# A two-layer graph network on one core: seams rearranged, the first linear layer one product later, adjacency transposes spread out

## The chip, the core and the metric

The kernel runs on one core of a Trainium2 chip. The core has five engines that run at the same time, each with its own queue: TensorE (PE) for matrix products, VectorE (DVE), ScalarE (ACT) and GpSimd (POOL) for elementwise work, SyncE (SP), which here only issues DMAs. They meet at semaphores. PE writes into PSUM, eight banks of 128 partitions x 512 fp32 numbers; everything else lies in SBUF or in device memory. The metric is the time of one launch in microseconds (us); lower is better.

## What is computed

Sixteen batches b of x (1024 nodes x 256 features), one adjacency matrix (1024 x 1024), all fp32, two layers. Cut from the reference:

```python
# layer 0
fea = transpose(x); c = mean(x, axis=features); diff = c[None, :] - c[:, None]
A = abs(abs(sigmoid(diff) - 0.5) - 0.5) * 2.0        # 1024 x 1024 per batch
g = relu((fea @ (adj * A_s)) * para)                  # A_s: A made symmetric
q = transpose(g); k, v = split(x @ kv_w)              # 4 heads of 64
x = layernorm(x + softmax(q @ k.T * scale) @ v)
# layer 1
A_hat = D^-1/2 (adj + I) D^-1/2
agg = A_hat-weighted sum of x over the nodes
h = relu(batchnorm(agg @ W1.T + b1))                  # 256 -> 512
o = batchnorm(h @ W2.T + b2)                          # 512 -> 256
x = layernorm(x + o)
```

The batch norms of layer 1 take their statistics over all batches and nodes. So the first linear layer must be done for all sixteen batches before the second starts, and the second for all before the final layernorm.

## The kernel before

`fast_path` does all the work, in stages that follow each other on PE:

- **Prologue.** Batch 0 is transposed, and keys, values and the row of node means are formed. `prologue(b)` returns three lists of closures (`first`, `steps`, `side`): `first` begins with `begin` (on DVE `csum`, `ccol`, `ncol`; two DMAs on SP that bring the means back as a row `crow`) and goes on with four transposes of x (`transpose_x`); `steps` holds the key and value products (L864, L877), and `side` the graph weights (L808, L813, L817).
- **Attention.** Sixteen batches of sixteen *bursts* (u = 0 to 15, about 3.4 us of PE each). A burst is two units of scores (`ps`, L924), exponentials on ACT (L929), and the outputs (`po`, L945) of the burst before. Between the bursts, lists called `sums` (`normalise`), `full` (`residual`), and `late` (`statistics_x1`, `finish_x1`: the layernorm) are drained at fixed values of u, and so is the next batch's prologue. In the last batch there is no next prologue; the dictionary `last` puts the preparation of layer 1 in its place: `transpose_adjacency(m, h)` (four transposes into a PSUM tile `pah`, copied by ACT into `ahT`, L1071 and L1074), `degrees`, `transpose_weights` (`pw`), `add_identity`, `scale_adjacency` (DVE, L1096).
- **`aggregate_first`** (L1123) aggregates batch 0 right after, into two PSUM tiles `pagg`. PSUM in this stage has tiles of three kinds, `tile_s` (two banks), `tile_t` and `tile_o` (one bank each).
- **Layer 1 loop**, b = 1 to 15: `aggregate(b)` and `linear1(b-1)` are interleaved on PE. Both go by a scheme of Strassen and Winograd with seven products instead of eight. `products` writes them as p1, p6, p2, p7, p5, p4, p3 on three PSUM banks a, b and c: p1 and p2 share bank a, p6, p7 and p4 share b, p5 and p3 share c. A later product accumulates onto what lies in its bank, after ACT or DVE has read the former value out. Aggregation has one such group of seven products per batch (3.43 us of PE each), linear has two (0.86 us a product) and statistics (L1382) after each group. The scheme needs sums of its operands beforehand: `x1_sums` makes `x1S` on POOL (L684 to L687) for the aggregation of two batches on, and `linear1(b)` first of all makes `tT` on DVE (`right_sums`, L691 to L694) from the finished `agg`.
- **Last linear**, `ph` (L1452), then the coefficients of the first batch norm, and `scale_shift1` (ACT, L1442), which applies it in place to `h`.
- **Second linear**, `po` (L1512): h is read back from device memory by `load_h` (L1497), two buffers `hl`. Evacuated by DVE (L1523), with statistics (L1527); the last tile by ACT (L1518).
- **Final stage**: `scale_shift` (ACT, L1554), the residual added on PE and DVE (L1563, L1577, L1592), statistics on DVE, the layernorm's coefficients on POOL (L1613), and `finish` (ACT, L1625, and DVE), then the output DMA (L1629).

The order on PE, ACT and DVE is written out by hand (`manual_schedule`): instructions stand in each engine's queue in the order in which Python emits them. POOL's and SP's are placed by the framework's scheduler. The loop that sets the order of layer 1:

```python
steps = aggregate(b)
for i, step in enumerate(steps):
    step()
    if i == len(steps) - 1 and b < B - 1:
        later = linear1(b)
    run_linear(lin, 2)
lin = later
```

`run_linear(lin, k)` emits the next k linear products; statistics and the store of h (POOL) come with the product that they follow. With two a step, steps 0 to 6 get p1 p6 | p2 p7 | p5 p4 | p3 p1 | p6 p2 | p7 p5 | p4 p3.

Of the kernel before, what the change touches and what calls it, by code (L numbers as in the profile page):

```python
# [18 lines left out]
P = 128  # L19
# [496 lines left out]
def fast_path(  # L516
# [208 lines left out]
    with (  # L725
# [235 lines left out]
        def normalise(b, pr):  # L961


            k = b * PAIRS + pr
            den = tile_t(f"den_{k}")
            for i in range(4):
                nc.tensor.matmul(  # L967
                    den[i * 32 : (i + 1) * 32, :], ones[:, :32],
                    G[b, pr, i // 2]["acc"][:, (i % 2) * HALF : (i % 2 + 1) * HALF],
                    start=True, stop=True,  # L970
                )
            row = rdp.tile([P, HALF], F32, tag="drow", name=f"drow_{k}")
            nc.scalar.copy(row, den)
            for i in range(4):
                nc.sync.dma_start(den_d[k][i : i + 1, :], row[i * 32 : i * 32 + 1, :])
            for qh in range(2):
                col = small.tile([P, 4, 2], F32, tag="dcol", name=f"dcol_{k}_{qh}")
                for hd in range(2):
                    i = 2 * qh + hd
                    nc.sync.dma_start(  # L980
                        col[:, :, hd], den_d[k][i : i + 1, :].rearrange("o (n p) -> p (o n)", p=P)
                    )
                G[b, pr, qh]["col"] = col

        def residual(b, pr, qh):
            g, s = G.pop((b, pr, qh)), st[b]
            k = (b * PAIRS + pr) * 2 + qh
            nc.vector.reciprocal(r_all[:, k], g["col"])
            pt = tile_t(f"poT_{k}")
            for j in range(4):  # L990
                nc.tensor.transpose(
                    pt[:, j * P : (j + 1) * P], g["oT"][:, j * P : (j + 1) * P], ident
                )
            o = rdp.tile([P, 4, 2, D], F32, tag="o", name=f"o_{k}")
            nc.vector.tensor_mul(  # L995
                o, pt.rearrange("p (n h d) -> p n h d", h=2, d=D),
                r_all[:, k].unsqueeze(3).to_broadcast([P, 4, 2, D]),
            )
            xs = s["x"][:, 4 * qh : 4 * qh + 4, pr * P : (pr + 1) * P]
            nc.gpsimd.tensor_tensor(xs, xs, o.rearrange("p n h d -> p n (h d)"), ALU.add)  # L1000
# [116 lines left out]
        def aggregate_first(m):  # L1117
            if m == 0:
                agg[0] = xTp.tile([P, CC, N], F32, tag="xT", name="agg_0")
                agg["ps"] = [tile_s(f"pagg_{c}") for c in range(CC)]  # L1120
            for c in range(CC):
                for hs in (H0, H1):
                    nc.tensor.matmul(  # L1123
                        agg["ps"][c][:, hs], x1l[0][:, m, c * P : (c + 1) * P], aht[m][:, hs],
                        start=(m == 0), stop=(m == NCH - 1),
                    )
            if m == NCH - 1:
                for c in range(CC):
                    nc.scalar.copy(agg[0][:, c, :], agg["ps"][c])
# [11 lines left out]
        with tc.manual_schedule(engines={mybir.EngineType.PE, mybir.EngineType.Activation, mybir.EngineType.DVE}):  # L1141
# [5 lines left out]
            for _ in range(8):  # L1147
                run(steps, 1)
                run(side, 2)
            run(next_first, 5)  # L1150
# [5 lines left out]
            run(next_side, 99)  # L1156
            run(next_steps, 8)
            full, sums, late = [], [], []

            def back(j):  # L1160
# [12 lines left out]
            last = {  # L1173
                0: [(transpose_adjacency, (m, h)) for m in (0, 1) for h in (0, 1)],
                4: [(transpose_adjacency, (m, h)) for m in (2, 3) for h in (0, 1)],
                6: [(transpose_adjacency, (m, h)) for m in (4, 5) for h in (0, 1)],
                8: [(transpose_adjacency, (m, h)) for m in (6, 7) for h in (0, 1)],
                5: [(load_x1l, (0,))],
                7: [(load_x1l, (1,))],
                9: [(degrees, ())],  # L1180
                10: [(transpose_weights, ())],
                12: [(add_identity, ())],
                15: [(scale_adjacency, (0,))],
            }
            before_last = {
                6: [(load_weights, ())],
# [7 lines left out]
            for j in range(len(bursts)):  # L1194
# [11 lines left out]
                if b == B - 1:  # L1206
                    if u == 0:
                        run(sums, 1)
                    elif u in (2, 4, 12):
                        run(full, 2)  # L1210
                    elif u == 5:
                        run(late, 1)
                    elif u == 7:
                        run(late, 1)
                    elif u == 8:
                        run(sums, 1)
                elif u == 0:
# [34 lines left out]
            for m in range(NCH):  # L1252
                if m + 1 < NCH:
                    scale_adjacency(m + 1)
# [5 lines left out]
            for i in range(NCH // 2):  # L1260
                adjacency_sums(i)
            run(late, 2)
# [24 lines left out]

    with (
# [5 lines left out]
        tc.manual_schedule(  # L1294
            engines={mybir.EngineType.PE, mybir.EngineType.Activation, mybir.EngineType.DVE}
        ),
# [118 lines left out]
        for b in range(1, B):  # L1415
            if b + 1 < B:
                load_x1l(b + 1)
                x1_sums(b + 1)
            else:
# [6 lines left out]
            for i, step in enumerate(steps):  # L1426
# [3 lines left out]
                run_linear(lin, 2)  # L1430
# [17 lines left out]
        for k in range(HC):  # L1448
            ps = [bank(f"ph_{k}_{half}") for half in range(2)]
            for c in range(CC):  # L1450
                for half, hs in enumerate((H0, H1)):
# [4 lines left out]
            if k == HC - 1:  # L1456
                scale_shift1(h0[0], 0)
# [6 lines left out]
        for k in range(1, HC):  # L1464
# [10 lines left out]
    with tc.tile_pool(name="o2p", bufs=1) as o2p:  # L1475
# [11 lines left out]
        with (  # L1487
            tc.tile_pool(name="hl", bufs=2) as hl,
            tc.manual_schedule(
                engines={mybir.EngineType.PE, mybir.EngineType.Activation, mybir.EngineType.DVE}  # L1490
            ),
        ):
            hs_of = {0: h0}

            def load_h(b):
                ht = hl.tile([P, HC, N], F32, tag="hl", name=f"hl_{b}")
                nc.sync.dma_start(ht, h_d[b])  # L1497
                hs_of[b] = [ht[:, k, :] for k in range(HC)]

            load_h(1)  # L1500
            for b in range(B):
                if b + 2 < B:
                    load_h(b + 2)
                if b + 1 < B:
                    for k in range(HC):
                        scale_shift1(hs_of[b + 1][k], k)
                h = hs_of.pop(b)
                for c in range(CC):
                    ps = tile_s(f"po2_{b}_{c}")
                    for k in range(HC):  # L1510
                        for hs in (H0, H1):
                            nc.tensor.matmul(  # L1512
                                ps[:, hs], w2T[:, k, c * P : (c + 1) * P], h[k][:, hs],
                                start=(k == 0), stop=(k == HC - 1),
                            )
                    if b == B - 1 and c == CC - 1:
                        for hs in (H0, H1):
                            nc.scalar.activation(  # L1518
                                o2T[b][:, c, hs], ps[:, hs], AF.Identity,
                                bias=cols["b2"][:, c : c + 1],  # L1520
                            )
                    else:
                        nc.vector.tensor_scalar(  # L1523
                            o2T[b][:, c, :], ps, cols["b2"][:, c : c + 1], None, ALU.add
                        )
                    for half, hs in enumerate((H0, H1)):
                        nc.vector.bn_stats(bn2_st[:, c, 2 * b + half, :], o2T[b][:, c, hs])  # L1527
                    if b == B - 1:
                        coefficients2(c)
                if b >= B - 3:  # L1530
                    load_x1(b - (B - 3), xp, "x")
# [7 lines left out]
        with (  # L1539
            tc.tile_pool(name="fin2", bufs=4) as fin2,  # L1540
            tc.tile_pool(name="ps_held", bufs=3, space=PSUM) as ps_held,
            tc.tile_pool(name="ps_sum", bufs=2, space=PSUM) as ps_sum,
            tc.manual_schedule(
                engines={mybir.EngineType.PE, mybir.EngineType.Activation, mybir.EngineType.DVE}
            ),
        ):
            for b in range(3, 7):
                load_x1(b, fin2, "xf")
# [20 lines left out]
            def residual2(b):  # L1569
# [27 lines left out]
                for n in range(4, NCH):  # L1597
                    nc.vector.bn_stats(st[:, n, :], held[b][:, (n - 4) * C : (n - 3) * C])

# [3 lines left out]
                pool = nc.gpsimd  # L1603
# [7 lines left out]
                pool.tensor_tensor(rstd, var, mhalf, ALU.pow)  # L1611
# [4 lines left out]
            def finish(b, rstd, nmr):  # L1616
                xt, hx = xf.pop(b), held.pop(b)
                y = o2T[b].rearrange("p c n -> p (c n)").rearrange("p (n c) -> p n c", c=C)
                for n in (0, 1):
# [4 lines left out]
                for n in (4, 5, 6, 7, 2, 3):  # L1624
# [4 lines left out]
                nc.sync.dma_start(out[b].rearrange("(n p) c -> p n c", p=P), y)  # L1629
                if b + 7 < B:  # L1630
                    load_x1(b + 7, *((fin2, "xf") if 3 <= b < 7 else (xp, "x")))
# [5 lines left out]
            for b in range(B):  # L1637
                coeffs[b] = residual2(b)
                if b + 1 < B:
                    scale_shift(b + 1)  # L1640
                if b:
                    finish(b - 1, *coeffs.pop(b - 1))
            finish(B - 1, *coeffs.pop(B - 1))


# [41 lines left out]
```

## Time and profile before

| | us |
|---|---|
| median of 3 runs (2630.56 to 2632.49) | 2630.99 |
| the profiled execution | 2630.78 |
| its span on the trace | 2628.9 |
| PE busy, of the span | 2565.4 |
| DVE busy | 1515.3 |
| ACT busy | 1202.5 |
| POOL busy | 362.0 |

The stages begin on PE at about these times of the trace: attention 78 us, its last batch 1622, `aggregate_first` 1704, layer 1 loop 1736, last linear 2286, second linear 2300, final stage 2526; the last output lands at the end of the span. One batch of the layer 1 loop lasts about 36.4 us.

The profile is read in views. The list of waits names, for each engine, what ended its idle times: the waiting group, the group that released it, the total, the number of times, the longest. A timeline gives start, duration, engine, line, operation, output and inputs by the program's names, tile shape, and in brackets how long the engine had been idle before and who ended it. Successive matmuls overlap a little in their recorded durations, so their pitch (start to start) is what they cost. A window gives the busy time of the engines in a stretch, PE, PEld (weight loads), DVE, ACT, POOL in this order, then the granted clock of PE (1.00 is full), the share of DMA time and GB/s.

### The profile page before, as it was taken

How to read it: one execution, taken by the hardware profiler on the slowest of the kernel's cores; microseconds unless marked ns; L12 is line 12 of the kernel's file. 1: busy time of each engine (PE TensorE's matmuls, PEld its weight loads, DVE VectorE, ACT ScalarE, POOL GpSimd, SP SyncE). 2: the span in 40 equal slices, each digit the busy share in tenths (PEclk: the TensorE clock that was granted, in tenths of full speed). 3: DMA queues.
4: the chain of work that ended last, by engine and by line, in shares of the span. 5: the costliest groups of instructions: out<-in, count | busy, mean ns of one | idle time of the engine just before them, and what ended most of it. 6: DMA issues, size and time to landing. Idle time of an engine off the chain costs nothing.

```text
span 2628.9 us, 32328 instructions
## 1 busy us (share of the span) xinstructions
PE 2565.4 (98%) x13158; PEld 1130.2 (43%) x13158; DVE 1515.3 (58%) x1941; ACT 1202.5 (46%) x1479; POOL 362.0 (14%) x439
## 2 busy tenths in 40 slices
PE   8999999999999999999999999999999999999986
PEld 4443443444434434444344444344444444444455
DVE  4365665655756646556566466766565565533367
ACT  6365564664655646646656564511010110133358
POOL 0010110101101101011011010331221122000035
PEclk9999999999999999999999999999999999999999
DMA  4001101011011011010110110111221222253458
GB/s 144 1 9 41 33 10 41 17 25 33 10 41 33 9 41 31 12 41 2 41 33 9 41 49 2 41 65 80 96 96 64 96 80 96 96 216 142 153 197 300
DMA packets 134559, 168.98 MB, mean 64 GB/s; under 512 B 86784, under 2 KB 120064, under 8 KB 124032
## 3 DMA queue, kind: packets, MB, share of 16 engines
q1 hardware_dynamic: 129568, 116.47, 14.0%
q0 software_dynamic: 4832, 50.34, 4.6%
q8 instruction: 105, 1.72, 0.3%
q14 instruction: 54, 0.44, 0.1%
HBM read 99.36 MB, written 67.44 MB: 63 GB/s over the span
## 4 chain that ended last, share of the span: by engine, by line
PE 83%; DVE 8%; ACT 6%; issue 1%; DMA 1%; POOL 0%; DVEq 0%; POOLq 0%; ACTq 0%
PE ps L924 16%; PE pg L827 16%; PE po L945 16%; PE po L1512 8%; PE pv L877 5%; PE b_agg L1341 4%; PE c_agg L1341 4%; PE pk L864 3%; PE b_h L1373 2%; PE a_agg L1341 2%; PE c_h L1373 2%; ACT o L1625 1%; ACT o L1554 1%; PE pxT L788 1%; PE den L967 1%
## 5 line engine op out<-in xcount | busy, mean ns | idle before, releaser
L929 ACT ACTIVATE p<-ps 128x1024 f32<-128x1024 f32 x512 | 496.8, 1023 | 192.8 <-PE ps L924 161.7
L954 DVE TENSOR_TENSOR acc<-acc,p 128x1024 f32<-128x1024 f32 x384 | 484.7, 1262 | 126.9 <-ACT p L929 98.0
L924 PE MATMUL ps<-qT,kT 64*64 64x512 f32 x4096 | 490.6, 592 | 0.6 <-DVE qT L836 0.3
L945 PE MATMUL po<-p,v 64*64 64x512 f32 x4096 | 488.0, 589 | 0.0
L827 PE MATMUL pg<-wg,x 128*128 128x512 f32 x960 | 420.9, 594 | 0.0
L1000 POOL TENSOR_TENSOR x<-x,o 128x512 f32<-128x512 f32 x64 | 123.1, 1924 | 1173.5 <-DVE o L995 1173.5
L945 PEld LDWEIGHTS po<-p,v 64*64 64x64 f32 x4096 | 159.9, 133 | 280.2 <-issue 271.5
L827 PEld LDWEIGHTS pg<-wg,x 128*128 128x128 f32 x960 | 178.9, 190 | 221.5 <-issue 208.5
L924 PEld LDWEIGHTS ps<-qT,kT 64*64 64x64 f32 x4096 | 152.6, 133 | 282.7 <-issue 254.4
L1512 PE MATMUL po<-hl,w12T 128*128 128x512 f32 x512 | 222.0, 596 | 3.4 <-DVE bn_st L1527 2.7
L836 DVE SCALAR_TENSOR_TENSOR qT<-pg,para_s 128x1024 f32<-128x1024 f32 (+1 forms) x34 | 39.2, 1160 | 236.2 <-PE pg L827 235.0
L817 DVE SCALAR_TENSOR_TENSOR wg<-wg,adj_s 128x1024 f32<-128x1024 f32 x128 | 162.1, 1278 | 22.9 <-ACT wg L813 22.9
L1512 PEld LDWEIGHTS po<-hl,w12T 128*128 128x128 f32 x512 | 97.7, 191 | 127.7 <-issue 120.9
L808 ACT ACTIVATE wg<-crow,ccol 128x1024 f32<-128x1024 f32 x128 | 147.1, 1150 | 9.3 <-DMA crow<-c 9.3
L813 ACT ACTIVATE wg<-wg 128x1024 f32<-128x1024 f32 x128 | 136.2, 1065 | 1.7
L1442 ACT ACTIVATE hl<-hl,bn_sh,bn_sg 128x1024 f32<-128x1024 f32 x64 | 74.3, 1229 | 137.1 <-DMA hl<-h 125.2
L877 PE MATMUL pv<-kvw_s,xT 128*128 128x256 f32 x512 | 126.9, 391 | 8.3 <-ACT kT L868 8.3
L959 DVE TENSOR_TENSOR oT<-po,oT 128x512 f32<-128x512 f32 x64 | 44.2, 691 | 145.6 <-ACT oT L958 145.6
L864 PE MATMUL pk<-xT,kvw_s 128*128 128x512 f32 x256 | 121.7, 598 | 3.3 <-ACT v L882 3.3
L1523 DVE TENSOR_SCALAR o<-po,col_b 128x1024 f32<-128x1024 f32 x31 | 39.8, 1284 | 137.9 <-PE po L1512 137.9
L622 ACT ACTIVATE x<-x,nm_l,rs_l 128x256 f32<-128x256 f32 x128 | 64.6, 587 | 111.4 <-POOL nm_l L618 111.4
L877 PEld LDWEIGHTS pv<-kvw_s,xT 128*128 128x128 f32 x512 | 92.6, 189 | 52.2 <-ACT kT L868 27.5
(163 smaller groups left out, 2698.0 us busy)
## 6 DMA issues: line engine op xcount, KB each, us to landing
h<-hw POOLq DMA_DIRECT2D x16, 2048.0 KB, 6.6
hl<-h SPq DMA_DIRECT2D x15, 2048.0 KB
x<-x POOLq DMA_DIRECT2D x16, 1024.0 KB, 4.2
x1l<-x SPq DMA_DIRECT2D x16, 1024.0 KB
xf<-x SPq DMA_DIRECT2D x16, 1024.0 KB
out_dram<-o SPq DMA_DIRECT2D x16, 1024.0 KB
x<-in_x_dram SPq DMA_DIRECT2D x15, 1024.0 KB
crow<-c SPq DMA_DIRECT2D x15, 512.0 KB
```

Source lines behind the costliest of these rows:

```text
L808: nc.scalar.activation(w, s["crow"], AF.Abs, bias=s["ccol"][:, n : n + 1])
L813: nc.scalar.activation(w, w, AF.Tanh, scale=0.5)
L817: nc.vector.scalar_tensor_tensor(w, w, 1.0, adj_s[:, n, :], op0=ALU.subtract, op1=ALU.mult)
L827: nc.tensor.matmul(s["pg"][:, hs], xt[:, n, c * P : (c + 1) * P], s["wg", n][:, hs], start=(n == 0), stop=(n == NCH - 1),)
L864: nc.tensor.matmul(ps, kvw_s[:, c, kc * P : (kc + 1) * P], s["xT"][:, c, hs], start=(c == 0), stop=(c == CC - 1),)
L877: nc.tensor.matmul(pt[:, j * C : (j + 1) * C], s["xT"][:, c, n * P : (n + 1) * P], kvw_s[:, c, C : 2 * C], start=(c == 0), stop=(c == CC - 1),
L924: nc.tensor.matmul(ps[kh * D : (kh + 1) * D, hd * HALF : (hd + 1) * HALF], kT[r, pr, ks], qT[r, pr, qh * HALF : (qh + 1) * HALF], start=Tr ...
L929: nc.scalar.activation(p, ps, AF.Exp)
L945: nc.tensor.matmul(g["po"][kh][hd * D : (hd + 1) * D, :], s["v"][r, m, h * D : (h + 1) * D], p[r, hd * HALF : (hd + 1) * HALF], start=(m = ...
L954: nc.vector.tensor_add(g["acc"], g["acc"], p)
L1341: nc.tensor.matmul(ps, left, right, start=(start and i == 0), stop=(i == NCH // 2 - 1), skip_group_check=True,)
L1512: nc.tensor.matmul(ps[:, hs], w2T[:, k, c * P : (c + 1) * P], h[k][:, hs], start=(k == 0), stop=(k == HC - 1),)
```

## The change

- **Start:** the first step of batch 1's prologue comes after the fifth of eight iterations, not after the loop; `next_steps` and `next_side` alternate at the end.
- **Last attention batch:** one group of adjacency transposes (two halves) in each of the first eight bursts; the other preparations move, four of the eight `scale_adjacency` come before the end of the bursts, and the rest with three `adjacency_sums` between the parts of `aggregate_first`. `den` and `poT` of the last pair take tiles of the kind s, the sums of `aggregate_first` take four single banks (kinds o and t), c = 1 first. The layernorm of the last batch is split: its statistics at the end of the stage, `last_apply` (ACT) inside layer 1's first batch, after which `x1l` of batch 2 is loaded and summed.
- **Layer 1:** linear's products come one step later: none at step 0, three at steps 1 and 6, two elsewhere: – | p1 p6 p2 | p7 p5 | p4 p3 | p1 p6 | p2 p7 | p5 p4 p3. One `manual_schedule` now spans layer 1 to the end.
- **Last linear and second linear:** the halves of `ph` are finished one after the other; `scale_shift1` of the first h goes with the coefficients one by one; the pool `hl` is placed first; the first batch goes over k in two halves; the last tile goes half by half.
- **Final stage:** the residual's x1 of batches 3 to 6 and 10 to 13 is loaded in pairs into `hl` buffers; for the last batch the coefficients, except the power, are on DVE, `finish` of the batch before is emitted between, DVE takes four of eight parts and ACT four, and the output leaves in two halves on SP's and ACT's queues.

```diff
@@ start
-            for _ in range(8):
+            for i in range(8):
                 run(steps, 1)
                 run(side, 2)
-            run(next_first, 5)
+                if i == 4:
+                    run(next_first, 1)
+            run(next_first, 4)
...
-            run(next_side, 99)
-            run(next_steps, 8)
+            for _ in range(8):
+                run(next_steps, 1)
+                run(next_side, 1)
@@ last attention batch
-            last = {
-                0: [(transpose_adjacency, (m, h)) for m in (0, 1) for h in (0, 1)],
-                4: [(transpose_adjacency, (m, h)) for m in (2, 3) for h in (0, 1)],
-                6: [(transpose_adjacency, (m, h)) for m in (4, 5) for h in (0, 1)],
-                8: [(transpose_adjacency, (m, h)) for m in (6, 7) for h in (0, 1)],
-                5: [(load_x1l, (0,))],
-                7: [(load_x1l, (1,))],
-                9: [(degrees, ())],
-                10: [(transpose_weights, ())],
-                12: [(add_identity, ())],
-                15: [(scale_adjacency, (0,))],
-            }
+            last = {u: [(transpose_adjacency, (u, h)) for h in (0, 1)] for u in range(NCH)}
+            for u, todo in (
+                (1, (load_weights,)), (6, (load_x1l, 0)), (9, (degrees,)), (11, (transpose_weights,)),
+                (12, (add_identity,)), (13, (load_x1l, 1)), (14, (scale_adjacency, 0)),
+                (14, (scale_adjacency, 1)), (15, (scale_adjacency, 2)), (15, (scale_adjacency, 3)),
+            ):
+                last.setdefault(u, []).append((todo[0], todo[1:]))
...
-                    elif u in (2, 4, 12):
+                    elif u in (2, 9, 13):
                         run(full, 2)
-                    elif u == 5:
-                        run(late, 1)
-                    elif u == 7:
-                        run(late, 1)
...
+                    elif u == 11:
+                        run(late, 1)
+                    elif u == 12:
+                        run(late, 1)
...
-                if m + 1 < NCH:
-                    scale_adjacency(m + 1)
+                if m == 0:
+                    for k in range(4, NCH):
+                        scale_adjacency(k)
+                elif m < 4:
+                    adjacency_sums(m - 1)
+                elif m == 4:
+                    adjacency_sums(3)
                 aggregate_first(m)
...
-            for i in range(NCH // 2):
-                adjacency_sums(i)
-            run(late, 2)
+            late.clear()
+            x_last = st.pop(B - 1)["x"]
+            last_statistics, last_apply = layernorm_steps(x_last, f"l0_{B - 1}")
+            last_statistics()
@@ layer 1
-            if b + 1 < B:
+            if 1 < b < B - 1:
                 load_x1l(b + 1)
                 x1_sums(b + 1)
-            else:
+            elif b == B - 1:
...
-                run_linear(lin, 2)
+                if i:
+                    run_linear(lin, 3 if i in (1, 6) else 2)
+                if b == 1 and i == 0:
+                    last_apply()
+                    nc.gpsimd.dma_start(x1_d[B - 1], x_last)
+                    load_x1l(2)
+                    x1_sums(2)
@@ second linear
-    with tc.tile_pool(name="o2p", bufs=1) as o2p:
+    with tc.tile_pool(name="hl", bufs=2) as hl, tc.tile_pool(name="o2p", bufs=1) as o2p:
@@ final stage
+                if b == B - 1:
+                    between()
...
-                pool = nc.gpsimd
+                pool = nc.vector if b == B - 1 else nc.gpsimd
...
-                pool.tensor_tensor(rstd, var, mhalf, ALU.pow)
+                nc.gpsimd.tensor_tensor(rstd, var, mhalf, ALU.pow)
...
-                for n in (0, 1):
+                last = b == B - 1
+                for n in (0, 1, 2, 3) if last else (0, 1):
...
-                nc.sync.dma_start(out[b].rearrange("(n p) c -> p n c", p=P), y)
+                dst = out[b].rearrange("(n p) c -> p n c", p=P)
+                if last:
+                    nc.sync.dma_start(dst[:, M0, :], y[:, M0, :])
+                    nc.scalar.dma_start(dst[:, M1, :], y[:, M1, :])
```

## The prediction

> **What bounds the kernel now.** I read the page's busy shares first, then the list of what TensorE (PE) waited for, then the timeline of one batch border of layer 1, engine by engine, and last the granted clock in the stretches after the longest waits.
>
> The page:
>
> ```profile
> PE 2565.4 (98%) x13158; PEld 1130.2 (43%) x13158; DVE 1515.3 (58%) x1941; ACT 1202.5 (46%) x1479; POOL 362.0 (14%) x439
> PEclk9999999999999999999999999999999999999999
> ```
>
> PE is busy for 2565.4 of 2628.9 us, so 63.5 us of PE idleness is all that reordering can win, start and end included. A new PE wait is paid in full.
>
> The waits of PE (total, times, longest):
>
> ```profile
> PE pv L877 <- ACT kT L868: 8.3, 29, 1.6
> ...
> PE po L1512 <- DVE bn_st L1527: 2.7, 1, 2.7
> ...
> PE pah L1071 <- DVE o L995: 1.9, 1, 1.9
> PE b_h L1373 <- DVE tT L692: 1.8, 1, 1.8
> ```
>
> No row is a large one. Each is a seam, except small ones that recur. In layer 1 the batch border is the place to look at. Its timeline, PE, then VectorE (DVE), then GpSimd (POOL):
>
> ```profile
> 2208.40 3.60 PE L1341 MATMUL c_agg<-ahT,x1S 128*128 128x512 f32 x8
> 2211.83 1.02 PE L1373 MATMUL b_h<-tT,w12T 128*128 128x512 f32 x2
> 2212.69 1.02 PE L1373 MATMUL c_h<-agg,wS 128*128 128x512 f32 x2
> 2213.55 3.60 PE L1341 MATMUL a_agg<-ahT,x1l 128*128 128x512 f32 x8
> ```
> ```profile
> 2208.60 0.69 DVE L671 TENSOR_TENSOR hw<-c_h,u_h 128x512 f32<-128x512 f32 x1
> 2212.03 0.69 DVE L679 TENSOR_TENSOR agg<-c_agg,u_agg 128x512 f32<-128x512 f32 x1 [2.74 <-PE c_agg L1341]
> 2212.76 1.15 DVE L691 TENSOR_TENSOR tT<-agg 128x512 f32<-128x512 f32 x1
> 2213.94 1.64 DVE L692 TENSOR_TENSOR tT<-agg,tT 128x512 f32<-128x512 f32 x1
> 2215.50 1.75 DVE L693 TENSOR_TENSOR tT<-agg 128x512 f32<-128x512 f32 x1
> 2217.17 1.75 DVE L694 TENSOR_TENSOR tT<-agg,tT 128x512 f32<-128x512 f32 x1
> 2218.85 0.74 DVE L640 SCALAR_TENSOR_TENSOR hw<-b_h,col_b,p_h 128x512 f32<-128x512 f32 x1
> ```
> ```profile
> 2212.09 1.26 POOL L684 TENSOR_TENSOR x1S<-x1l 128x512 f32<-128x512 f32 x1 [27.24 <-PE c_agg L1341]
> ...
> 2216.78 1.59 POOL L687 TENSOR_TENSOR x1S<-x1l,x1S 128x512 f32<-128x512 f32 x1
> ```
>
> What to see: when the last aggregation product (c_agg) ends, DVE adds it up and forms four tT sums in a row, until 2218.9. PE meanwhile runs on without a gap. It may, because DVE read linear's p5 out of bank c_h (L671) at 2208.60, before c_agg ended, so p3, which accumulates onto that bank, finds it read at 2212.69. And the sums are slow (1.15 to 1.75 us) because POOL's four x1S sums start on the same event; a batch later, with no POOL sums left, L691 to L694 start at 2249.19 and take 0.69, 0.69, 0.68 and 0.68 us.
>
> The granted clock, in windows of 3.4 us that begin at most 1.5 us after waits of 1.92, 2.67 and 2.32 us:
>
> ```profile
> 30.60:34.00 3.40, 3.40 (x9) 1.85 (x8) 2.96 (x3) 2.53 (x3) 0.00 (x0) 0.51 0.10 6
> 2317.60:2321.00 3.40, 3.40 (x5) 1.32 (x5) 0.00 (x0) 3.21 (x4) 0.00 (x0) 0.50 0.96 410
> 2532.60:2536.00 3.40, 3.40 (x16) 3.40 (x17) 2.08 (x6) 3.40 (x4) 0.00 (x0) 0.50 1.00 424
> ```
>
> Column PEclk (third from the right) is one half. Waits of 1.90, 1.78 and 1.63 us had no such window behind them.
>
> **What the Trainium skill says.** "TensorE: Matmul & The Clock Gate", Part 1, says that an idle window of about 3.4 us halves the clock until PE has been busy for about 3.4 us. The three windows agree on the second number; here waits of 1.92 us and more already did it, so I use the trace. Its section "Architectural detail: the array is 16× 32×32, not 1× 128×128" calls DVE and ACT strict first-in-first-out; the DVE rows above, in their written order behind a busy engine, agree. "SBUF — State Buffer", "SBUF: two separate sides", says a DVE operation with two SBUF inputs and a GpSimd operation lock each other out of a shared port pair; 0.69 us against 1.75 us beside x1S agrees.
>
> **Layer 1, the large term.** In the change, linear runs no product at aggregation step 0, three at steps 1 and 6, two elsewhere. So step 6 now holds the second group's p5, p4 and p3 together, and they are emitted after linear1(b), which puts the four tT sums into DVE's written order first. DVE's order becomes: L679 of agg, L691, L692, L693, L694, then L671, which reads p5. PE's p3 must wait for this L671, and behind p3 on PE stands a_agg of the next batch: nothing else can fill the gap.
> With the rows above: without a wait p3 would start after p5 and p4 (0.86 us pitch each, 2211.83 to 2212.69) at 2211.83 + 1.72 = 2213.55. L694 ends when the next DVE row starts, 2218.85; L671 takes 0.69, to 2219.54; some 0.06 for the semaphore: 2219.60. The wait is 6.05 us. POOL's sums fall on the same event for b = 1 to 13 (they make x1S of b + 2): 13 x 6.05 = 78.7. For b = 14 the sums end at about 2251.81, L671 at 2252.50; p3's free start is 2249.98, a wait of 2.6. At b = 15 there is no linear1(b). Sum 81.3.
> Clock: after each of these 14 waits 3.4 us run at half speed, which is 1.7 us lost: 14 x 1.7 = 23.8. Bounds: 0 (clock never falls) and 3.4 (twice as long cold). I take 1.7, since all three waits above 1.9 us show it.
> What it gains: with linear one product later, b_h no longer waits for DVE's late tT in the steady batches. Their period is 36.42 us (c_agg at 2208.40 and at 2244.83) against 36.05 of PE work: 0.37 x 12 = 4.4. p1, p6 and p2 in a row at step 1 is safe: ACT's copy of p1 takes 0.58 and starts 0.25 after p1's end (2234.53, 2234.78), about the 0.86 of p6.
> Layer 1 net: +81.3 + 23.8 - 4.4 = +100.7.
>
> **Start.** The first step of batch 1 (its column sums, 2.27 us of DVE, and the DMAs of its means on SP) comes after the fifth step of the prologue's loop, not after the eighth; keys and sides are interleaved. PE's waits at 27.43 (0.24), 30.01 (1.92, with about 1.5 of half clock behind it) and for kT (1.63) shrink; the sums now stand before two copies on DVE. I take -3.0 (-2.4 to -3.9).
>
> **Last attention batch to layer 1.** Two adjacency transposes a burst instead of four every few bursts: each finds its PSUM buffers free, as ACT has 3.4 us a burst for two copies. Waits removed, from the PE timeline 1626 to 1736: 0.29, 1.90, 0.78, 0.34, 1.15, 0.19, 0.35, 1.33, 0.23, 1.10 = 7.7, and in batch 1 1.78 and 1.50 = 10.9 in all. New ones: pah behind residual's o and a copy (1.8 at two places, as 1.90 was), pw behind the statistics of batch 14 on DVE (1.35), scores behind ACT's normalisation of batch 14 (1.3), aggregate_first's first bank behind DVE's oT, itself behind four scalings of 1.28 us (3.1), a_h behind last_apply on ACT, which waits for POOL (1.0), and small ones of 0.6: 9.2. Net -1.7 (-4 to +1.5).
>
> **First to second linear.** SP issued hl_1 at 2308.12: the buffers lay over those of the h stores. Now hl has memory of its own, allocated first, and hl_1 waits for the store of h_1 and the last aggregation alone, so it lands before 2312. PE's 2.67 goes, and the half clock behind it (61 po matmuls took 28.14 us there, 26.2 later: 1.9): -4.6. The po that waits for ACT's hw L1459 (0.8) stays.
>
> **End.** The wait of 2.32 at 2528.8 stays: ACT's two halves of the last o still wait for the last matmul. The final stage is ACT's, 5.06 us a batch. For the last batch the statistics leave POOL but for the power (POOL ran 4.1 us there), but DVE does finish(14) first (-0.3); ACT has 4 instead of 6 activations at its end (1.09 of L1625); the output goes in two halves on two queues. I take -1.3.
>
> **Sum.** 100.7 - 3.0 - 1.7 - 4.6 - 1.3 = +90.1 on a span of 2628.9, so 2719.0; with the 1.9 us outside the span (2630.78 - 2628.9) 2720.9, say 2720. The profiled execution is 0.2 below the median, so the median needs no correction.
>
> **Rivals.**
> A: the wait comes, the clock stays. For it: waits of 1.90 and 1.78 didn't cost clock. Against: three longer ones did. 2720 - 24 = 2696.
> B: the sums are served quickly (POOL's x1S shifts, 0.69 each): 14 x (2.6 + 1.7) = 60 instead of 105, 2675. Against: POOL's row is released by the very c_agg that releases L679.
> C, the other side: the wait doesn't decide. L671 is done before p4 ends, within 1.72 us of c_agg's end; this needs p5's read ahead of the four sums on DVE. Then only the gains count: 4.4 + 3.0 + 1.7 + 4.6 + 1.3 = 15, 2616. For it: the change means well everywhere else, and 0.90 us of L679 plus 0.69 would just fit. Against: DVE has no instruction out of order in any timeline.
> D: the cold stretch doubles, 14 x 1.7 more: 2744.
>
> **How the numbers follow.** Forecast 0.80, A 0.08, B 0.03, C 0.05, D 0.04. Range 2695 to 2734: it takes in A's clock and an error of 1 us in each wait. 0.2%, which is 5.3 us, is about what a measurement can tell from no change. Faster is C, 0.05; within 0.2% would need C with its gains lost, 0.01; slower 0.94.
>
> **What would show it.** PE's list gets a row "c_h L1373 <- DVE hw L671", about 80 us in 14 times, longest 6.1, and the timeline repeats some 43.8 us apart in layer 1 (36.4 before), with PE at half clock for 3.4 us after each wait. The row "po L1512 <- DVE bn_st" is gone. I am wrong if layer 1 still takes 36 us a batch, or if another engine than DVE releases p3.

## The result and the profile after

The changed kernel takes 2736.26 us (median of 4 runs, 2735.66 to 2737.10) against 2630.96 before: ratio 1.0399, 95% interval 1.0381 to 1.0417. Its profiled execution took 2736.06, with a span of 2734.2, which is 105.3 more than before. The forecast was 2720 with a range up to 2734: the direction and the main mechanism were right, the size was 16 us short.

The page of the changed kernel, busy times and granted clock:

```profile
PE 2595.9 (95%) x13158; PEld 1138.8 (42%) x13158; DVE 1518.8 (56%) x1952; ACT 1201.3 (44%) x1479; POOL 356.3 (13%) x430
PEclk9999999999999999999999999999999999999999
```

PE executes the same 13158 matmuls, but is busy for 30.5 us more (2565.4 before): the same work on a slower clock. The row of tenths can't show it; it needs windows. The waits of PE in the changed kernel (total, times, longest):

```profile
PE c_h L1385 <- DVE hw L671: 78.3, 14, 5.8
...
PE pagg L1127 <- DVE oT L959: 6.4, 1, 6.4
PE pw L1052 <- DVE w12T L1046: 6.1, 1, 6.1
```

The first row is the forecast's large term; before, it didn't exist. The other two are new too, and the stage in which they lie makes up most of the missing 16 us. The batch border in layer 1, for the changed kernel, PE, DVE and POOL:

```profile
2043.97 1.02 PE L1385 MATMUL c_h<-tT,wS 128*128 128x512 f32 x2
2044.83 1.02 PE L1385 MATMUL b_h<-tT,w12T 128*128 128x512 f32 x2
2051.70 2.08 PE L1385 MATMUL c_h<-agg,wS 128*128 128x512 f32 x2 [5.84 <-DVE hw L671]
2053.57 4.77 PE L1353 MATMUL a_agg<-ahT,x1l 128*128 128x512 f32 x8
2058.17 3.60 PE L1353 MATMUL b_agg<-aT,x1S 128*128 128x512 f32 x8
```
```profile
2044.17 0.69 DVE L679 TENSOR_TENSOR agg<-c_agg,u_agg 128x512 f32<-128x512 f32 x1 [2.68 <-PE c_agg L1353]
2044.90 1.14 DVE L691 TENSOR_TENSOR tT<-agg 128x512 f32<-128x512 f32 x1
2046.08 1.63 DVE L692 TENSOR_TENSOR tT<-agg,tT 128x512 f32<-128x512 f32 x1
2047.63 1.74 DVE L693 TENSOR_TENSOR tT<-agg 128x512 f32<-128x512 f32 x1
2049.30 1.74 DVE L694 TENSOR_TENSOR tT<-agg,tT 128x512 f32<-128x512 f32 x1
2050.97 0.68 DVE L671 TENSOR_TENSOR hw<-c_h,u_h 128x512 f32<-128x512 f32 x1
```
```profile
2044.23 1.26 POOL L684 TENSOR_TENSOR x1S<-x1l 128x512 f32<-128x512 f32 x1 [33.00 <-PE c_agg L1353]
...
2048.91 1.59 POOL L687 TENSOR_TENSOR x1S<-x1l,x1S 128x512 f32<-128x512 f32 x1
```

Read it from the right: p3 (c_h at 2051.70) starts when DVE's L671 is done; L671 has nothing to wait for (p5 ended at about 2044.8) but stands behind four sums; the sums are slow beside POOL. p4 has a pitch of 0.86 and would have left PE at 2045.69, so the wait is 6.01 us (the list's 5.84 counts from p4's modelled end). Then c_h and a_agg need 6.47 us (2051.70 to 2058.17) where 0.86 + 3.43 = 4.29 would do: 2.18 us go to the clock. It is seen in windows of the same border; the last three columns are the granted clock, the share of DMA, and GB/s:

```profile
2047.00:2049.00 2.00, 0.00 (x0) 0.00 (x0) 2.00 (x2) 0.00 (x0) 1.92 (x3) 1.00 0.00 0
2049.20:2051.70 2.50, 0.00 (x0) 0.00 (x1) 2.50 (x4) 0.00 (x0) 1.30 (x1) 0.50 0.00 0
2051.70:2055.80 4.10, 4.10 (x5) 1.85 (x6) 2.59 (x5) 0.00 (x0) 0.57 (x1) 0.50 0.00 0
2056.00:2060.00 4.00, 4.00 (x11) 1.82 (x10) 0.88 (x2) 0.59 (x1) 0.00 (x0) 1.00 1.07 451
```

The clock falls to one half while PE still waits, and stays there for 4.2 us of work.

By stage, from the starts of the same instructions on PE in both profiles, the final stage from the end of the second linear's last product (us; the forecast's parts are put into the stage in which they fall, so that the two seam waits of batch 1 count in layer 1):

| stage | before | after | difference | forecast |
|---|---|---|---|---|
| start, up to the second unit of scores | 78.1 | 73.2 | -4.9 | -3.0 |
| attention, batches 0 to 14 | 1548.9 | 1549.2 | +0.3 | 0 |
| last attention batch, first aggregation | 109.6 | 121.1 | +11.5 | +0.5 |
| layer 1 loop and last linear | 564.1 | 669.0 | +104.9 | +98.4 |
| second linear | 224.6 | 220.0 | -4.6 | -4.6 |
| final stage | 103.6 | 101.7 | -1.9 | -1.3 |
| sum | 2628.9 | 2734.2 | +105.3 | +90.0 |

### The profile page after: what moved, and what is told of

Read it like the earlier page. It is cut to its first block, busy times and chain, and to the rows that moved or that the text cites. A ratio compares the mean times of both kernels' runs of the same rounds, so it can differ in the third digit from the quotient of the medians.

```text
span 2734.2 us, 32320 instructions
## 1 busy us (share of the span) xinstructions
PE 2595.9 (95%) x13158; PEld 1138.8 (42%) x13158; DVE 1518.8 (56%) x1952; ACT 1201.3 (44%) x1479; POOL 356.3 (13%) x430
## 4 chain that ended last, share of the span: by engine, by line
PE 86%; DVE 6%; ACT 5%; issue 1%; DMA 1%; POOL 0%; POOLq 0%; DVEq 0%; ACTq 0%
PE ps L924 15%; PE pg L827 15%; PE po L945 15%; PE po L1523 8%; PE b_agg L1353 6%; PE a_agg L1353 4%; PE pv L877 4%; PE c_agg L1353 4%; PE pk L864 3%; PE b_h L1385 2%; PE c_h L1385 2%; PE a_h L1385 2%; ACT o L1661 1%; ACT o L1587 1%; PE pxT L788 1%
## 5 line engine op out<-in xcount | busy, mean ns | idle before, releaser
L1353 PE MATMUL a_agg<-ahT,x1l 128*128 128x512 f32 x240 | 125.1, 669 | 0.7 <-ACT agg L1134 0.7
L1385 PE MATMUL c_h<-agg,wS 128*128 128x512 f32 x60 | 44.6, 835 | 78.3 <-DVE hw L671 78.3
L648 ACT COPY p_agg<-a_agg 128x512 f32<-128x512 f32 x15 | 8.8, 586 | 249.6 <-PE a_agg L1353 249.6
```

Of the source, the lines that this page charges most:

```text
L1353: nc.tensor.matmul(ps, left, right, start=(start and i == 0), stop=(i == NCH // 2 - 1), skip_group_check=True,)
L1385: nc.tensor.matmul(ps, left, right, start=start, stop=True, skip_group_check=True)
```

## The experiments

Ratios stand against runs of the kernel before on the same chip. It took 2631.3 us beside e1 to e4, 2632.0 beside e5 to e8, 2630.7 beside e9 and 2630.3 beside e10, so that a comparison of two medians from different groups carries up to 1.7 us of the chip.

**Only the order of DVE's queue (e1).** The changed kernel, with the four sums emitted behind linear's last products:

```diff
-                if i == len(steps) - 1 and b < B - 1:
-                    later = linear1(b)
                 if i:
                     run_linear(lin, 3 if i in (1, 6) else 2)
+                if i == len(steps) - 1 and b < B - 1:
+                    later = linear1(b)
```

> The changed kernel with linear1(b), and so the four tT sums, emitted after the three linear products of step 6. Theory (p3 waits only because DVE's read of p5 stands behind the four sums): the 14 waits of c_h vanish, the batch goes from 44.37 us to about 36.2, 13 x 8.2 plus 4 for the last one: 2736 - 110 = about 2626 us. Rival (DVE is too late with tT in any order, one product's shift is the cause): the sums now end 4.5 us later, b_h waits for tT instead, and the time stays above 2650 us.

Measured: 2628.44 us, ratio 0.9989 (0.9980 to 0.9998). The row of c_h is gone from the list of waits. The same border in e1, PE and DVE:

```profile
2106.46 1.02 PE L1385 MATMUL b_h<-tT,w12T 128*128 128x512 f32 x2
2107.41 1.12 PE L1385 MATMUL c_h<-agg,wS 128*128 128x512 f32 x2
2108.37 3.60 PE L1353 MATMUL a_agg<-ahT,x1l 128*128 128x512 f32 x8
```
```profile
2106.66 0.69 DVE L671 TENSOR_TENSOR hw<-c_h,u_h 128x512 f32<-128x512 f32 x1 [0.17 <-PE c_h L1385]
...
2111.56 0.67 DVE L691 TENSOR_TENSOR tT<-agg 128x512 f32<-128x512 f32 x1
...
2113.48 0.69 DVE L694 TENSOR_TENSOR tT<-agg,tT 128x512 f32<-128x512 f32 x1
```

L671 now follows p5 by 0.17 us, p3 comes 0.95 us after p4 instead of 6.9, and the sums, which are in nobody's way 5.0 us later, come after POOL's, which end at 2110.9 here, and take 0.7 us. A steady batch lasts 36.37 us. One move of two lines takes 107.8 us (2736.26 - 2628.44) away. The rival (DVE too late in any order) falls.

**The shift alone (e2).** The kernel before, with the changed kernel's counts for `run_linear` and nothing else:

```diff
-                run_linear(lin, 2)
+                if i:
+                    run_linear(lin, 3 if i in (1, 6) else 2)
```

> The kernel before with nothing changed but linear's products one step later. Theory: the shift alone makes nearly the whole loss: 13 x (6.0 + 2.2) + 4.2 for the waits and their clock, less 4.4 and 3.3 for the waits it removes: about +103, 2734 us. Rival (the other parts share in it, as by the new schedule's bounds or by loads): clearly less, under 2715 us.

Measured: 2735.19 us, ratio 1.0398 (1.0380 to 1.0415). The shift makes the whole loss by itself.

**All but the shift (e4).** The changed kernel with two products a step, as before (the edit of e2 the other way round).

> The changed kernel with linear's products where they were, two a step. Theory: the batch is back at 36.4 us, and what is left of the change (start -4.9, last attention batch and first aggregation +11.5, second linear -4.6, end -1.9) nets to nothing: about 2631 us. Rival (the other parts win as forecast, 15 us less 4.4): 2620 us; or they cost: over 2637 us.

Measured: 2628.74 us, ratio 0.9990 (0.9981 to 0.9999): 2.5 us faster. The stage differences other than layer 1's add up to +0.4, and layer 1 was 562.2 in this kernel against 564.1, as its wait for tT in batch 1 is gone too. So the rest of the change, meant in four places, nets to hardly anything, because one place loses what the others win.

**POOL beside DVE, and the clock (e3).** The changed kernel with a tiny POOL operation ahead of the x1S sums of a batch, which reads the last statistics of the linear group before, so that the sums can't start with tT:

```diff
             x1S[b] = strs.tile([P, 4, NCH // 2, P], F32, tag="x1S", name=f"x1S_{b}")
+            if after is not None:
+                nc.gpsimd.tensor_scalar(
+                    x1S[b][:, 0, 0, 0:1], bn1_st[:, HC - 1, 2 * after + 1, 0:1], 0.0, None, ALU.add
+                )
```

> The changed kernel with POOL's x1S sums made to wait for the statistics of the linear group before, so that they no longer run beside the tT sums. Theory: tT takes 0.69 a sum, the wait of c_h falls from 6.0 to 2.5 us in 14 times. With a clock loss of 1.7 us after each wait the batch takes about 40.3 us: 2736 - 53 = 2683. Rival on the clock (the release comes at the ends of free-running windows of about 3.41 us, and 44.37 is 13 of them): the batch locks to 12 windows, 40.96 us, 2692 us, or the waits of 2.5 us are often unpunished, 38.7 us and 2662. Rival on POOL (sums slow for another reason): the wait stays 6 us and the time at 2736.

Measured: 2690.12 us, ratio 1.0224 (1.0206 to 1.0241). DVE in e3:

```profile
2025.99 1.13 DVE L691 TENSOR_TENSOR tT<-agg 128x512 f32<-128x512 f32 x1
2027.15 0.69 DVE L692 TENSOR_TENSOR tT<-agg,tT 128x512 f32<-128x512 f32 x1
2027.77 0.68 DVE L693 TENSOR_TENSOR tT<-agg 128x512 f32<-128x512 f32 x1
2028.37 0.68 DVE L694 TENSOR_TENSOR tT<-agg,tT 128x512 f32<-128x512 f32 x1
```

Three sums are quick; L691 still meets one POOL sum (L686, which doesn't write where the tiny operation wrote, and so wasn't held back). The wait by pitch is 2.93 us (2026.78 to 2029.71). So 3.1 of the 6.0 us of each wait are POOL's doing, and 46 of the 105 us of loss went with them. The clock of the same border:

```profile
2029.70:2030.90 1.20, 1.19 (x3) 0.68 (x4) 0.64 (x2) 0.00 (x0) 0.00 (x0) 1.00 0.00 0
2031.10:2034.30 3.20, 3.20 (x5) 1.33 (x4) 2.84 (x5) 0.00 (x0) 0.83 (x2) 0.50 0.38 164
2034.60:2038.00 3.40, 3.40 (x10) 1.49 (x9) 0.00 (x0) 0.58 (x1) 3.24 (x3) 1.00 0.94 400
```

Here the half clock comes 1.3 us after the wait and lasts 3.4 us: 1.8 us lost (c_h and a_agg 6.09 instead of 4.29), near the forecast's 1.7. The time doesn't choose between the theories: it is within 2 us of 2692, and 2683 assumed a wait of 2.5 where it was 2.93, which makes 2689. The trace does. The steady period was 40.91 us and not the 40.96 of a lock at 12 windows, so the wait slid by 0.05 us a batch against the half clock that followed it; and the tenth wait (2149.51 to 2152.44), as long as the others, had no half clock behind it:

```profile
2150.00:2152.40 2.40, 0.00 (x0) 0.00 (x0) 2.40 (x5) 0.00 (x0) 0.00 (x0) 1.00 0.00 0
2153.00:2156.00 3.00, 3.00 (x9) 1.33 (x8) 2.44 (x6) 0.00 (x0) 0.62 (x1) 1.00 0.00 0
```

The next batch came after 39.21 us. The last section says what set this wait apart.

**A wait in between (e8).** Three of the four sums ahead of linear's last products, the fourth behind them:

```diff
-                nc.vector, [tT[:, i, :] for i in range(4)],
...
+            nc.vector.tensor_tensor(T[0], b12, b11, ALU.subtract)
+            nc.vector.tensor_tensor(T[1], b22, T[0], ALU.subtract)
+            nc.vector.tensor_tensor(T[2], b22, b12, ALU.subtract)
...
                     run_linear(lin, 3 if i in (1, 6) else 2)
+                if fourth_sum:
+                    fourth_sum.pop()()
```

> The changed kernel with three of the four tT sums ahead of linear's last products and the fourth behind them: the wait of c_h should be 4.3 us instead of 6.0. With a fixed loss of 1.7 us per wait the batch takes 42.2 us: 2708 us. With a half clock that lasts whole windows of 3.41 us from a free-running start, the unthrottled 40.5 us and the loss depend on the phase: near 12 windows (40.96 us a batch) 2692 us, and the losses differ from batch to batch.

Measured: 2712.29 us, ratio 1.0304 (1.0287 to 1.0321). The wait is 4.3 us by pitch at each of the first 13 borders, yet the periods come to alternate: c_h starts at 2040.35, 2083.62, 2125.74, 2168.97, 2211.08, which is 43.27, 42.12, 43.23, 42.11 apart. Windows of two successive borders of e8 tell why:

```profile
2039.00:2040.30 1.30, 0.00 (x0) 0.00 (x0) 1.30 (x3) 0.00 (x0) 1.22 (x2) 0.50 0.00 0
2040.30:2045.50 5.20, 5.15 (x6) 2.19 (x7) 3.69 (x7) 0.00 (x0) 1.09 (x2) 0.50 0.19 79
...
2083.30:2086.50 3.20, 2.88 (x4) 1.34 (x5) 1.69 (x4) 0.00 (x0) 0.78 (x1) 0.50 0.00 0
2086.80:2090.00 3.20, 3.20 (x9) 1.40 (x8) 2.59 (x5) 0.30 (x1) 0.57 (x1) 1.00 0.67 282
```

Equal waits, unequal punishment: at the first border half clock for over 6.5 us, 1.5 us of it in the wait; at the second for little over 3.2, nearly all of it at work. Cut into slices of 0.5 us (a slice that is partly half and partly full gives the moment), it lasts from 2038.87 to 2045.69, 6.82 us, and from 2083.24 to 2086.65, 3.41 us. The time is near the 2708 of a fixed loss per wait, but losses that differ by 1.1 us after equal waits are no fixed loss; a lock at 12 windows (2692) didn't come either: the mean period is 42.7.

**The last attention batch (e5, e6, e7, e9).** On top of e1. First, the two new waits of the changed kernel as its DVE shows them. Ahead of pw's copy (L1046):

```profile
1674.15 3.88 DVE L954 TENSOR_TENSOR acc<-acc,p 128x1024 f32<-128x1024 f32 x3
1677.95 0.42 DVE L614 BATCH_NORM_STATS2 st_l<-x 128x6 f32<-128x256 f32 x1
...
1681.66 0.39 DVE L614 BATCH_NORM_STATS2 st_l<-x 128x6 f32<-128x256 f32 x1
...
1682.19 1.25 DVE L1046 COPY w12T<-pw 128x512 f32<-128x512 f32 x2
```

and ahead of the last oT, which holds pagg's bank:

```profile
1705.34 3.41 DVE L1100 SCALAR_TENSOR_TENSOR ahT<-ahT,dg,dinv_row 128x1024 f32<-128x1024 f32 x2
1708.67 3.94 DVE L954 TENSOR_TENSOR acc<-acc,p 128x1024 f32<-128x1024 f32 x2
1712.54 0.68 DVE L959 TENSOR_TENSOR oT<-po,oT 128x512 f32<-128x512 f32 x1
```

PE was ready for pw's second part at 1676.8 and for pagg's at 1706.9. Both times the transposed or finished tile waits for DVE's backlog. At the second, two acc additions of 1.97 us instead of 1.26 (POOL forms wS and x1S then) make it worse. The edits:

```diff
 e5  (11, (transpose_weights,))  ->  (10, (transpose_weights,))
 e6  scale_adjacency 1, 2, 3 at u = 14, 15  ->  after the bursts, with 4 to 7
 e7  both, and linear's counts  3 if i in (2, 6) else 2
 e9  e7 with transpose_weights at u = 8, statistics of batch 14 at u = 10
```

> The kernel e1 with transpose_weights one burst earlier in the last attention batch (u = 10 instead of 11), so that DVE's copies of pw stand before the statistics of batch 14 and not behind them. Theory: PE's wait of pw for w12T falls from 6.1 us to about 0.4 and takes its half clock (about 2 us) with it: 2628.4 - 7.5 = 2621 us. Rival (DVE's backlog of acc additions, not the statistics, holds the copies): the wait shrinks by less than half, 2626 us or more.

Measured: 2626.22 us, ratio 0.9977 (0.9968 to 0.9986). The wait shrank to less than half, but the gain is 2.2 us. PE's waits in e5:

```profile
PE ps L924 <- ACT p L929: 3.8, 2, 3.5
PE pagg L1127 <- DVE oT L959: 3.8, 1, 3.8
...
PE pw L1052 <- DVE w12T L1046: 2.7, 1, 2.7
```

The wait of ps, 1.4 in the changed kernel, has grown to 3.8: ACT normalises batch 14 at a fixed place, waits there for POOL and so for the statistics on DVE, and the exponentials stand behind it.

> The kernel e1 with only scale_adjacency(0) ahead of the end of the bursts, and 1 to 7 after DVE's last oT. Theory: three scalings of 1.2 to 1.7 us leave the place ahead of oT, the wait of pagg falls from 6.4 us to about 1.8, and the half clock behind it (1.7) goes: 2628.4 - 6.3 = 2622 us. Rival (the sums on POOL at this place make DVE late anyway): the wait falls by less than 3 us, 2626 us or more.

Measured: 2623.28 us, ratio 0.9966 (0.9953 to 0.9978): -5.2, as expected within 1.1. The wait for oT fell to 1.5, and one of 1.3 for ahT came.

> The kernel e1 with both repairs, and linear's counts 2, 3, 2, 2, 2, 3 for steps 1 to 6, so that p2 no longer follows p6 at once behind ACT's copy of p1. Theory: the gains add up (7.5 + 6.3), and 0.12 us in each of 15 batches more (1.8): 2628.4 - 15.6 = about 2613 us, which beats both kernels. Rival (a wait removed in the last attention batch comes back later in the same stage): 2620 us or more.

Measured: 2618.04 us, ratio 0.9948 (0.9931 to 0.9964), 10.4 below e1 where 15.6 had been expected. It beats both kernels. Waits of 3.6 (ps) and 2.7 (pw) are left, as in e5.

> The kernel e7 with the weights' transposes at u = 8 and the statistics of batch 14 at u = 10, so that both stand ahead of the burst in which ACT normalises batch 14 (u = 12). Theory (in e7 DVE's statistics came too late, so ACT's normalisation waited for POOL and the exponentials behind it made PE wait 3.6 us): the wait of ps falls from 3.6 to about 1, that of pw from 2.7 to 0.5, with the half clock behind it: 2618 - 6.5 = about 2611.5 us. Rival (DVE has a backlog of about 4.3 us wherever the statistics stand, and another wait takes their place): 2616 to 2619 us.

Measured: 2618.01 us, ratio 0.9949 (0.9935 to 0.9963). pw no longer waits, and nothing is won: ps now waits 4.4 us in three places and pagg 2.8. The rival was right: the 4.3 us of statistics fall in a stage in which DVE has little to spare, and moving them moved the wait.

**Everything but that stage (e10).** All the other parts of the change, linear's order as in e7, and the last attention batch and first aggregation as in the kernel before.

> All of the change except its rearrangement of the last attention batch and the first aggregation, which are as before, with linear's reads of p5 ahead of the sums as in e7. By the stages' times: start -4.9, layer 1 -4 to -5 (steady wait and the wait for tT in batch 1 gone), second linear -4.6, end -1.9: 2631 - 15.5 = 2615.5 us. That is 2.5 us below e7 and would put the rearranged stage, even repaired, at a loss. Rival (the stage's wait for x1 and the scalings of before cost as much once layer 1 is faster): 2618 us or more.

Measured: 2614.20 us, ratio 0.9942 (0.9928 to 0.9955): 16.1 us faster than before, the lowest of all, and within 1.3 us of what the stages had promised. Its ratio and e7's lie within each other's intervals; the traces tell the two apart: the stage takes 109.6 us in e10, as before, and 113.2 in e7.

## Why the prediction was right or wrong

Of the 15.3 us that the sum of the stages missed, 11.0 lie in the last attention stage and 6.5 in layer 1; the start and the end won 2.5 more than forecast.

**The wait of p3: right.** Engine, instruction, place, number (14) and size were as worked out: 6.01 us against 6.05, 2.48 against 2.6 at b = 14, 80.6 us in all against 81.3. e1 and e2 show that the order of L671 and the sums on DVE is the cause, by taking it away and by making it alone. e3 shows that POOL's part of it is half. Rival C needed just e1's two lines; its 2616 became 2628 by the loss of the last attention stage, and in e10, which has that stage as before, it is 2614.

**The clock: right in kind, too small in size.** "14 x 1.7 = 23.8" is the term. Behind the 14 waits, c_h and a_agg took 30.7 us more in all than 4.29 each, 2.2 us a wait. I took 1.7 from waits of 1.9 to 2.7 us, each followed by one stretch of 3.4 us at half speed. After a wait of 6 us there are two such stretches, with 2.6 us of them inside the wait, which costs nothing: (6.8 - 2.6) / 2 = 2.1. That is rival D's doubled stretch, less its part in the wait. At b = 14, where the wait was 2.48, the loss was 1.8, as the short waits had shown. My upper bound, 3.4, covered it, and the chosen value didn't.

**The last attention batch: the step that failed.** "New ones: ... 9.2. Net -1.7" was wrong by the largest amount: the stage lost 11.5 us where my parts give +0.5. Two items of that sum were mis-sized. pw was put at 1.35 and measured 6.1: I let the statistics of batch 14 start with the burst, but three acc additions stood before them, so that pw paid for all of it. The wait for oT was put at 3.1 and measured 6.4, since I counted the scalings at their undisturbed 1.28 us and forgot that POOL slows acc as well. And I charged no clock to this stage, though waits of 6 us must pay it by the very rule I used for layer 1: the granted clock was 0.57 over 1682.9 to 1688.0 and 0.65 over 1713.3 to 1720.0, which is some 2.2 and 2.4 us. My bounds for this part (-4 to +1.5) came from the small waits seen before, not from the backlog of the queue. e5, e6 and e7 show that these two waits are worth taking away, and e9 and e10 that the stage's new order, in the forms tried, isn't worth having.

**p2 is not quite safe.** I called p1, p6, p2 in a row safe. In the trace p6 to p2 (2062.47 to 2063.35) and p2 to a_agg (2064.31) take 0.88 and 0.96 us instead of 0.86 each: 0.12 a batch, 1.8 in all. e7's counts, which part p2 from p6, took 2.1 us out of layer 1 (560.8 us in e1, 558.7 in e7). p3 is not quite free either: in e1 it starts 0.95 us after p4, and a_agg 0.96 after it. So the gain of 4.4 in the steady batches was too large: the period, 36.42 before, is 36.37 in e1 and 36.24 in e7, which over 12 batches is 0.6 and 2.2.

**The other seams: right, with the start too small.** The second linear gained 4.6 as forecast, the end 1.9 against 1.3. The start gained 4.9 against 3.0. Some 1.1 of it is due to faster first matmuls (the row of means took 3.60 instead of 4.39 us, the transposes 3.45 instead of 3.84), which is chance and not the change: the row of means took 3.60 us in e2, which has the old start, and 4.49 in e3, which has the new one. Why these first matmuls differ isn't shown; the granted clock reads full in both. Kernels with like first matmuls differ by 4.1 (before 78.1, e3 74.0) and 4.3 (e2 77.4, e10 73.1).

**The 63.5 us of PE idleness** were not all that reordering could win. In e10 PE's busy time, too, is 5.1 us less than before (2560.3), 3.4 of it from the two stretches of half clock at 30.65 and 2317.58, which went with their waits.

**The range** reached to 2734. It should have held an error of 11 us in the attention stage and a clock loss of 2.2.

## What to carry to other kernels

When work is moved by one place in a hand-written order, list for every product that accumulates onto a used bank which instruction reads the bank out, and what stands ahead of that reader on its engine; the cost is the whole queue ahead, not the reader's own 0.7 us. Emit readers that release TensorE before sums that only a later product needs. Price each wait of over two microseconds with its clock, everywhere, and price a wait on an engine with little slack by its backlog, not by the waits that the profile shows today.

## What the runs showed of the hardware

The half clock comes in whole pieces of 3.41 us, which lie on one grid that runs on regardless of the work. In e3 there is one such piece at the border shown (2031.00 to 2034.42), in the changed kernel two (2049.09 to 2055.9), in e8 two and one in turn; the starts at 2038.87 and 2083.24 in e8 are 44.37 apart, which is 13 pieces. In the kernel before, which has no such loop of waits, the starts at 2317.58 and 2532.62 are 215.04 apart, which is 63. The Trainium skill, "TensorE: Matmul & The Clock Gate", "What's actually happening", gives a free-running window of 3413 ns, which these numbers agree with; that such a window must be idle throughout before the clock falls they don't bear out.

What counted was PE's idle time inside one piece of the grid, however long the whole wait was. In e3 the tenth wait, 2.93 us like its neighbours, had 1.97 us in the piece that ended at 2153.88, and no half clock followed; the ninth had 2.02 us in the piece that ended at 2112.92, and half clock followed. Over the full-clock pieces of all twelve traces (without the first 10 and the last 20 us of each, and by the ends of matmuls that the traces record), 1.87 us of idle time or less was never followed by half clock, 1.98 or more always, and between them (1.90 to 1.97) it went both ways. A piece at half clock was followed by another when PE idled for 0.61 us or more in it, and by full clock when it idled for 0.42 or less. That is why a wait of 6 us, with 2.6 us in its second piece, has two. In the kernel before, the wait of 1.90 us cost no clock since only 1.63 of it lay in one piece; the wait of 1.92 did, with 0.2 of an earlier one in the same piece.

The loop of the changed kernel falls into step with that grid. Its batches came 44.57, 44.69 and 44.32 us apart at first, and from then on 44.34 to 44.38: 13 x 3.413 = 44.37. A wait that ends later leaves less of its half clock to the work, so the next batch comes sooner (at 1829.62 4.44 us were left and 2.5 lost, at 1874.31 4.12 and 2.1). In e3 the whole piece falls into the work, nothing pulls the loop back, and it drifts. Two turns of e8 make 85.3, 25 pieces. So the loss per wait is not set by the wait's length alone: 1.8 us or nothing for 2.93, 1.6 and 2.7 in turn for 4.3 (the periods less 40.52 of work and waiting), 2.2 for 6.01.
